# First token group of a four-layer graph network: one uninterrupted run of norm steps, row-sum products behind the first mix, 16 more unread products

## The chip, the cores and the metric

The kernel runs on one core of one Trainium2 chip. The metric is device time in microseconds (us), the median of the runs shown. All tensors are float32.

## The reference

There are 128 graphs of 64 nodes with 256 features each, `x[128, 64, 256]`, and one 64 x 64 matrix `adj` for all. Four layers follow each other; each adds a function of `relu(layernorm(x))` to `x`. Cut to what matters here:

```python
# layer 0: two graph convolutions, then LSTMs over windows of 1, 2, 3 and 4 nodes
h = relu(layernorm(x))
h = relu(einsum('ts,bsh->bth', adj, h @ Wg0 + bg0))
h = relu(einsum('ts,bsh->bth', adj, h @ Wg1 + bg1))
for p in 1..4:
    h[:, every p-th node] = lstm_last(Wih[p-1], Whh[p-1], windows of p nodes of h)
x = x + h
# layer 1: graph convolution with 2*adj/lmax(adj) - I, attention over the nodes, MLP
# layer 2: graph attention; layer 3: two projections between U.T and U,
#          U the eigenvectors of the normalised Laplacian of adj
```

The bias of a graph convolution goes through `adj` too: it reaches an output node multiplied with that node's row sum of `adj`. Layers 1 and 3 need the largest eigenvalue and all eigenvectors of 64 x 64 matrices, which the kernel computes itself.

## The kernel before

**Tiles and groups.** The 8192 node rows are 64 token tiles of 128 rows (two graphs) by 256 features. Layer 0 takes them in 8 groups of 8 tiles (`GT = 8`) and stores each result in DRAM (`put`). Layers 1 to 3 take them in 16 groups of 4 tiles (`HT = 4`). The eigenvalue work (`EIG`, on tiles of `arena`) depends on no tokens and is laid between the groups' work.

**What sets the order.** Every operation is first recorded by a planner (class `Plan`): engine, operands, what it depends on, an estimated cost (`cost`), the group it belongs to, and a `lead` that sets its rank. `schedule` then takes operation after operation, the earliest possible first and by rank among those that are ready, and `issue` writes each engine's program in that order. So every instruction of the program carries the line of `issue`, L349, in the profile, and a changed cost or a changed dependency can re-deal the order of all engines. `plan.burst(cost)` records what stands inside it as one operation, whose instructions stay together. `plan.behind = op` makes everything recorded after it depend on `op`. For operations that lock the port which VectorE and GpSimd share, `schedule` keeps a time of its own (`op.port`).

**How it starts.** The first group's two halves (`X0`, 4 tiles each) are fetched by ACT's DMA queue in pieces of one, one, two, two and two tiles. SP's queue brings `adjT2`, `adj2`, the weights `Wg`, biases and the LSTM's weights `Wih` and `Whh`. TensorE starts with products of a tile of ones with itself, whose results nothing reads: 6 into the bank `warm`, then 8 into the two `seed` banks. In the profile they are `bank<-ones` and `seed<-ones`.

**Row sums.** `rscol` is the row sum of `adj2`, by VectorE. Two products with `adjT2` (`bank<-adjT,ones` and `bank<-adjT,rscol`) put two rows of sums into the bank `rs`; VectorE copies them to `rsrow` and makes `C0T` (two instructions) and `B1T` (four) from them. `C0T` is first needed when a tile pair's second mix is written out, `B1T` after the product with `Wg[1]`.

**Layer 0's front.** The first group goes through in four pairs of tiles (`nl = 2`), the others in fours. For a pair: `ln_stats` (VectorE's `bn_stats` and `bn_aggr`, then four GpSimd instructions that make scale and shift in `stat`), Relu by ACT into `mids`, a mix (16 products of 64 x 64 blocks with `adjTb`, 32 records in the profile), two copies by ACT, four products with `Wg[0]`, a maximum with `nB0` by VectorE (`y`), a second mix, and four additions of `C0T` by VectorE into `big`. Then, for the whole group, eight products with `Wg[1]` (`bank<-big,Wg`, 512 columns), four maxima by VectorE and four additions of `B1T` by GpSimd; the LSTM steps (`bank<-big,Wih`) read their result. In the same time GpSimd makes sums of weight blocks (`sums`), 24 of them, for products that need seven block products in place of eight.

The four GpSimd instructions of `ln_stats` are recorded one by one:

```python
G.tensor_scalar(rs[:, 0, :], mv[:, :, 1], 1e-5, None, op0=ALU.add)
G.tensor_tensor(rs[:, 0, :], rs[:, 0, :], mhalf[:, :n], op=ALU.pow)
G.tensor_tensor(rs[:, 1, :], mv[:, :, 0], rs[:, 0, :], op=ALU.mult)
G.tensor_scalar(rs[:, 1, :], rs[:, 1, :], -1.0, None, op0=ALU.mult)
```

Of the kernel before, what the change touches and what calls it, by code (L numbers as in the profile page):

```python
# [1 line left out]

# [6 lines left out]
ALU = mybir.AluOpType  # L9
# [3 lines left out]
N = 64  # L13
# [55 lines left out]
class Plan:  # L69
# [110 lines left out]
    @staticmethod  # L180
    def cost(op, aps):

        def free(ap):
            n = 1
            for _, c in ap.ap[1:]:
                n *= c
            return n
        n = max(free(a) for a in aps)
        if op.name == "dma_start" and op.eng != "SP":
            return 0.6, 4.0  # L190
        if op.eng == "PE":
            n = free(aps[0])
            if op.name == "transpose":
                c = 0.11
            elif aps[0].ap[0][1] <= 64 and aps[1].ap[0][1] <= 64:
                c = 0.08
            else:
                c = 0.001672 * n + 0.006 if n >= 128 else 0.2
            return c, c + 0.22
        if op.eng == "V":  # L200
            if op.name == "bn_stats":
                c = 0.33
            elif op.name == "bn_aggr":
                c = 0.09
            elif op.name in ("tensor_copy", "tensor_scalar") and all(str(a.space) == "SB" for a in aps):
                c = 0.075 + 0.0006 * n + 0.05 * (len(aps) - 2)
            elif op.name == "reciprocal":
                c = 0.075 + 0.0065 * n
            elif op.name == "tensor_reduce" and aps[1].ap[-1][0] != 1:
                c = 0.075 + 0.0022 * n  # L210
            else:
                c = 0.075 + 0.00105 * n
            if "accum_out" in op.kw:
                c += 0.075
            return c, c + 0.12
        if op.eng == "ACT":
            c = 0.07 + 0.00082 * n + 0.1 * max(0, len(aps) - 2)
            if op.kw.get("func", op.args[2] if len(op.args) > 2 else None) is AF.Exp:
                c += 0.12
            return c, c + 0.15  # L220
        if op.eng == "G":
            c = 0.44 + 0.14 * n if op.kw.get("op") is ALU.pow else 0.12 + 0.00218 * n if n > 64 else 0.2
            return c, c + 0.05
        c = max(0.6, free(aps[0]) * aps[0].ap[0][1] * 4e-6 / 0.39)
        return c, c + 2.2
# [6 lines left out]
    def schedule(self):  # L232
# [20 lines left out]
        while len(order) < len(self.ops):  # L253
# [34 lines left out]
            ready[e].remove(op)  # L288
            tb = self.table(op)
            cost, lat = op.cost, op.lat  # L290
            if tb and tb != table:
                table, cost, lat = tb, cost + 1.29, lat + 1.29
# [603 lines left out]
P = 128  # L896
# [6 lines left out]
SETUP, WEIGHTS, ATTN, REST, EIG = -1, NG, NG + 1, NG + 2, 1000  # L903
# [109 lines left out]
def gnn_kernel(ctx: ExitStack, tc: tile.TileContext, a, out):  # L1013
# [4 lines left out]
    def C(shape, name):  # L1018
        return pool.tile(list(shape), F32, name=name)
# [45 lines left out]
    plan = Plan(tc, {"PE": nc.tensor, "V": nc.vector, "ACT": nc.scalar, "G": nc.gpsimd, "SP": nc.sync}, pools, late, reserve, window, EIG, REST + NT // HT - 6, slack)  # L1065
    PE, V, ACT, G, SP = (plan.proxy(e) for e in ("PE", "V", "ACT", "G", "SP"))

    def bank(name):
        return plan.value("bank")

    def load(t, src):
        SP.dma_start(t, src)
        return t
# [20 lines left out]
    adjT2 = C([P, N], "adjT2")  # L1094
# [9 lines left out]
    bgc = [load(C([P, 2], f"bgc{i}"), a[f"bg{i}"].rearrange("o (c p) -> p (o c)", p=P)) for i in range(2)]  # L1104
# [17 lines left out]
    ones = C([P, P], "ones")  # L1122
    V.memset(ones, 1.0)

    warm = bank("warm")
    for i in range(6):
        PE.matmul(warm[:, :P], ones, ones, start=True, stop=True)
    for i in range(2):
        seed = plan.value("seed")
        for j in range(4):  # L1130
            PE.matmul(seed[:, j * P:(j + 1) * P], ones, ones, start=j == 0, stop=True, skip_group_check=True)
    mhalf = C([P, HT], "mhalf")
    V.memset(mhalf, -0.5)

# [8 lines left out]

    rscol = C([P, 1], "rscol")
    V.reduce_sum(rscol, adj2, axis=AX.X)
    pb = bank("rs")
    PE.matmul(pb[:, :N], ones[:N], adjT2[:N], start=True, stop=True)
    PE.matmul(pb[:, N:2 * N], rscol[:N].to_broadcast([N, P]), adjT2[:N], start=True, stop=True)
    rsrow = C([P, 2, 2, N], "rsrow")
    V.tensor_copy(rsrow, pb[:, :2 * N].rearrange("p (r n) -> p r n", r=2).unsqueeze(2).to_broadcast([P, 2, 2, N]))  # L1150


    V.tensor_scalar(nB0, nB0, rscol, -1.0, op0=ALU.mult, op1=ALU.mult)
    C0T = C([P, 2, P], "C0T")
    B1T = C([P, 2, 2, P], "B1T")
    row = lambda r: rsrow[:, r].rearrange("p r n -> p (r n)")
    for c in range(2):
        V.tensor_scalar(C0T[:, c], row(1), bgc[0][:, c:c + 1], None, op0=ALU.mult)
        for t in range(2):
            V.tensor_scalar(B1T[:, t, c, :], row(0), bgc[1][:, c:c + 1], 1.0 if t else -1.0, op0=ALU.mult, op1=ALU.mult)  # L1160
    G.tensor_tensor(bl, bl, bh, op=ALU.add)


# [95 lines left out]
    def mix(src, m, nt, nc=2):  # L1259

        ps = [bank("mix") for i in range(2)]
        with plan.burst():
            for c in range(nc):
                for t in range(nt):
                    for i, r in ((0, 0), (0, 1), (1, 0), (1, 1)):
                        PE.matmul(ps[i][half(r), bat(c * nt + t)], src(t, c)[half(i), half(r)], m(t)[half(i), half(i)], start=True, stop=True)
        return [p[:, :nc * nt * N].rearrange("p (c t n) -> p c t n", c=nc, t=nt) for p in ps]
# [9 lines left out]
    def mid():  # L1279
        return plan.value("mid")  # L1280
# [8 lines left out]
    def ln_stats(src, n=HT):  # L1289

        s = plan.value("stat")
        st = s[:, :6 * n].rearrange("p (t k) -> p t k", k=6)
        mv = s[:, 6 * n:8 * n].rearrange("p (t k) -> p t k", k=2)
        rs = s[:, 8 * n:10 * n].rearrange("p (k t) -> p k t", k=2)
        for t in range(n):
            V.bn_stats(st[:, t, :], src[:, t, :])
            V.bn_aggr(mv[:, t, :], st[:, t, :])
        G.tensor_scalar(rs[:, 0, :], mv[:, :, 1], 1e-5, None, op0=ALU.add)
        G.tensor_tensor(rs[:, 0, :], rs[:, 0, :], mhalf[:, :n], op=ALU.pow)
        G.tensor_tensor(rs[:, 1, :], mv[:, :, 0], rs[:, 0, :], op=ALU.mult)  # L1300
        G.tensor_scalar(rs[:, 1, :], rs[:, 1, :], -1.0, None, op0=ALU.mult)
        return lambda t: rs[:, 0, t:t + 1], lambda t: rs[:, 1, t:t + 1]


# [106 lines left out]
    def layer0(fetched):  # L1411
# [5 lines left out]
        for t0 in range(0, GT, nl):  # L1417
            sc, bi = norms[t0 // nl]
            two = lambda t: t.rearrange("p (t f) -> p t f", t=2)
            h, ah, y = ([], [], [])  # L1420
            for j in range(0, nl, 2):
                h.append(two(mid()))
                for t in (j, j + 1):
                    ACT.activation(h[-1][:, t - j, :], x[(t0 + t) // HT][:, (t0 + t) % HT, :], AF.Relu, scale=sc(t), bias=bi(t))
            ps = mix(lambda t, c: h[t // 2][:, t % 2, tok(c)], lambda t: adjTb, nl)
            for j in range(0, nl, 2):
                ah.append(mid().rearrange("p (c t) -> p c t", c=2))
                for i in range(2):
                    ACT.copy(ah[-1].rearrange("p c (t b n) -> p c t b n", t=2, b=2)[:, :, :, i, :], ps[i][:, :, j:j + 2, :])
            for j in range(0, nl, 2):  # L1430
                yp = bank("y")
                for t in range(2):
                    for c in range(2):
                        PE.matmul(yp[:, t * D:(t + 1) * D], ah[j // 2][:, c, tok(t)], Wg[0][:, c, :], start=c == 0, stop=c == 1)
                y.append(two(mid()))
                V.tensor_tensor(y[-1], two(yp), vec(nB0, 2), op=ALU.max)
            ps = mix(lambda t, c: y[t // 2][:, t % 2, tok(c)], lambda t: adjTb, nl)
            part = ayT[t0 // HT][:, :, t0 % HT * P:(t0 % HT + nl) * P].rearrange("p c (t b n) -> p c t b n", t=nl, b=2)
            for i in range(2):
                for c in range(2):  # L1440
                    V.tensor_tensor(part[:, c, :, i, :], ps[i][:, c], vec(C0T[:, c, half(i)], nl), op=ALU.add)

        hT = [plan.value("big")[:, :P * GT] for m in range(2)]
        for hf in range(2):
            ts = slice(hf * GT // 2, (hf + 1) * GT // 2)
            for m in range(2):
# [3 lines left out]
                dst = hT[m].rearrange("p (n t) -> p n t", t=GT)[:, :, ts]  # L1450
                b1 = [B1T[:, i, m, :].unsqueeze(2).to_broadcast([P, P, GT // 2]) for i in range(2)]
                V.tensor_tensor(dst, ps.rearrange("p (t n) -> p n t", n=P), b1[0], op=ALU.max)
# [368 lines left out]
```

## Time and profile before

| | |
|---|---|
| median of 3 runs | 2100.99 us (2100.03 to 2101.82) |
| profiled execution | 2099.95 us, span 2098.2 us |
| instructions in the trace | 48166 |
| PE / PEld busy | 2065.2 us (98%) / 1678.8 us (80%) |
| DVE busy | 1767.8 us (84%) |
| ACT busy | 1097.0 us (52%) |
| POOL busy | 777.8 us (37%) |
| mean DMA rate | 28 GB/s |

PE is TensorE, PEld its weight loads, DVE is VectorE, ACT is ScalarE, POOL is GpSimd and SP is SyncE. The span runs from the first to the last instruction; 1.75 us of the execution lie outside it. A row of the timeline has the start in us, the busy time in us, engine, line, operation, what is written and read, shapes, and the number of instructions; in brackets stands how long the engine had been idle before it and what ended that. Buffer numbers are left out of the names, so `bank` is any of the PSUM banks. A matmul of float32 leaves two records. A busy time includes the way through the array, so that the distance between two starts tells more of the rate than a record's length does.

### The profile page before, as it was taken

Reading aid. Unit: us, or ns where it says so; the run is one execution under the profiler, and the core shown is the slowest. Engines: PE = TensorE matmul, PEld = TensorE weight load, DVE = VectorE, ACT = ScalarE, POOL = GpSimd, SP = SyncE. Lnnn points to the kernel's source line nnn. Section 1 sums busy time; section 2 is a strip of 40 time slices with the busy share of each in tenths; the row PEclk is TensorE's granted clock in tenths of the full one; section 3 lists DMA queues with packets and bytes.
Section 4 is the critical chain, followed back from the end, with each engine's and each line's share of the span. In section 5 each row is a group of like instructions: output and inputs, shape, how many; then the busy total and the mean of one; then the engine's idle time right before and its main releaser. Section 6 shows DMA issues by size and latency. Waiting matters only on the chain.

```text
span 2098.2 us, 48166 instructions
## 1 busy us (share of the span) xinstructions
PE 2065.2 (98%) x17928; PEld 1678.8 (80%) x17928; DVE 1767.8 (84%) x6691; ACT 1097.0 (52%) x2465; POOL 777.8 (37%) x1162
## 2 busy tenths in 40 slices
PE   8999999999999999999999999999999999999998
PEld 6689689689779778878878789987887788788776
DVE  7799899899999999999988954877878878885787
ACT  3344544544443453444444435575667666664674
POOL 7422221221211122022010123677557576854354
PEclk9999999999999999999999999999999999999999
DMA  6000100100100100000000211200100100000001
GB/s 231 1 3 3 63 2 2 62 2 2 61 1 1 61 2 1 21 26 2 30 12 1 98 44 33 82 2 1 42 22 1 35 29 22 12 12 11 2 1 62
DMA packets 44875, 57.84 MB, mean 28 GB/s; under 512 B 8928, under 2 KB 38496, under 8 KB 44640
## 3 DMA queue, kind: packets, MB, share of 16 engines
q1 hardware_dynamic: 43536, 53.71, 8.0%
q8 instruction: 141, 2.31, 0.5%
q10 hardware_dynamic: 1104, 1.05, 0.2%
q14 instruction: 94, 0.77, 0.1%
HBM read 37.53 MB, written 16.78 MB: 26 GB/s over the span
## 4 chain that ended last, share of the span: by engine, by line
PE 87%; DVE 10%; issue 1%; ACT 1%; POOL 0%; DMA 0%; DVEq 0%; ACTq 0%
PE bank L349 70%; PE seed L349 17%; DVE big L349 3%; DVE arena L349 3%; DVE stat L349 2%; DVE mids L349 1%; ACT mids L349 1%; DVE sums L349 1%; DMA big<-in_x_dram 0%; DVE seed L349 0%; POOL stat L349 0%; DVE Whh L349 0%; ACT big L349 0%; DVE bank L349 0%; DMA adjT<-in_adjT_dram 0%
## 5 line engine op out<-in xcount | busy, mean ns | idle before, releaser
L349 PE MATMUL bank<-big,Wih 128*128 128x512 f32 (+4 forms) x1800 | 552.1, 425 | 1.1 <-DVE big L349 0.7
L349 PEld LDWEIGHTS bank<-big,Wih 128*128 128x128 f32 x1800 | 315.4, 190 | 141.6 <-issue 95.9
L349 PE MATMUL bank<-big,sums 128*128 128x128 f32 (+3 forms) x1936 | 361.5, 301 | 5.8 <-DVE big L349 2.5
L349 ACT ACTIVATE mids<-bank,bl 128x512 f32<-128x512 f32 (+2 forms) x432 | 246.8, 576 | 206.3 <-PE bank L349 191.9
L349 PE MATMUL bank<-big,Whh 128*128 128x128 f32 (+3 forms) x1304 | 322.5, 333 | 1.4 <-ACT big L349 1.4
L349 PEld LDWEIGHTS bank<-big,sums 128*128 128x128 f32 (+1 forms) x1936 | 286.5, 188 | 40.8 <-issue 17.7
L349 DVE TENSOR_TENSOR arena<-arena 64x42 f32<-64x42 f32 (+6 forms) x1358 | 275.0, 230 | 18.6 <-POOL arena L349 0.3
L349 PEld LDWEIGHTS bank<-big,Whh 128*128 128x128 f32 x1304 | 215.3, 191 | 22.6 <-issue 10.7
L349 ACT ACTIVATE mids<-seed,bl 128x256 f32<-128x256 f32 (+2 forms) x192 | 102.1, 532 | 225.4 <-PE seed L349 223.2
L349 DVE TENSOR_TENSOR big<-mids 128x512 f32<-128x512 f32 (+2 forms) x256 | 154.7, 613 | 27.3 <-ACT mids L349 24.9
L349 POOL TENSOR_SCALAR stat<-stat 128x4 f32<-128x4 f32 (+1 forms) x236 | 70.7, 300 | 260.7 <-DVE stat L349 247.9
L349 PE MATMUL seed<-big,sums 128*128 128x128 f32 (+3 forms) x800 | 141.0, 299 | 0.0
L349 DVE SCALAR_TENSOR_TENSOR arena<-arena 64x1 f32<-64x1 f32 (+16 forms) x565 | 128.7, 251 | 10.6 <-ACT arena L349 3.5
L349 POOL TENSOR_TENSOR big<-big,B1T 128x512 f32<-128x512 f32 x32 | 37.8, 1186 | 255.1 <-DVE big L349 233.8
L349 ACT COPY seed<-bank 128x128 f32<-128x128 f32 (+2 forms) x192 | 53.8, 280 | 145.7 <-PE bank L349 143.8
L349 ACT ACTIVATE mids<-big 128x256 f32<-128x256 f32 (+2 forms) x176 | 89.4, 510 | 74.2 <-DVE big L349 71.5
L349 POOL TENSOR_TENSOR stat<-stat,mhalf 128x4 f32<-128x4 f32 (+1 forms) x118 | 126.2, 1069 | 5.2
L349 ACT COPY mids<-bank 128x256 f32<-128x256 f32 (+3 forms) x320 | 107.6, 357 | 38.7 <-PE bank L349 36.8
L349 POOL MEMSET arena<- 64x2 f32 (+5 forms) x72 | 7.8, 113 | 306.2 <-DVE arena L349 301.7
L349 PEld LDWEIGHTS seed<-big,sums 128*128 128x128 f32 (+1 forms) x800 | 115.8, 189 | 3.5 <-issue 0.3
L349 DVE TENSOR_SCALAR arena<-arena 64x1 f32<-64x1 f32 (+8 forms) x506 | 102.3, 211 | 6.8 <-POOL arena L349 0.3
L349 PE MATMUL seed<-big,Whh 128*128 128x128 f32 (+3 forms) x424 | 103.6, 326 | 0.3 <-DVE big L349 0.3
(507 smaller groups left out, 4615.9 us busy)
## 6 DMA issues: line engine op xcount, KB each, us to landing
big<-in_x_dram SPq DMA_DIRECT2D x29, 512.0 KB, 5.2
put<-big SPq DMA_DIRECT2D x15, 512.0 KB, 3.0
big<-put SPq DMA_DIRECT2D x9, 512.0 KB, 6.4
out_dram<-big SPq DMA_DIRECT2D x18, 256.0 KB, 2.3
Wih<-in_WihT_dram SPq DMA_DIRECT2D x3, 1024.0 KB, 12.0
Whh<-in_WhhT_dram SPq DMA_DIRECT2D x3, 1024.0 KB, 13.6
sums<-put SPq DMA_DIRECT2D x5, 512.0 KB, 4.1
out_dram<-sums SPq DMA_DIRECT2D x10, 256.0 KB, 2.2
```

The source lines that it names most:

```text
L349: getattr(self.engines[op.eng], name)(*map(real, args), **{k: real(a) for k, a in kw.items()})
```

## The change

1. The four GpSimd instructions of `ln_stats` are recorded as one operation in the first group (`plan.burst`, with an estimated cost of 1.04 + 0.14 n us), so that no other GpSimd instruction comes between them.
2. The two row-sum products, the copy to `rsrow` and the six instructions that make `C0T` and `B1T` move into a function `rows()`, which is called once, in the first group, right after the first pair's first mix, and whose operations depend on that mix. The scaling of `nB0` by `rscol` stays where it was.
3. After the 14 unread products 16 more are recorded, into the bank `warm`, with a low rank in group 0.
4. The estimated cost of a DMA that is not issued by SP becomes 0.5 us of issue and a time to landing that grows with its size; before it was 0.6 and 4.0 us for every size.

In the program that the planner makes, the 16 products stand directly behind the 14 and ahead of the first mix.

```diff
--- before.py
+++ after.py
@@ -1,4 +1,4 @@
-from contextlib import ExitStack, contextmanager
+from contextlib import ExitStack, contextmanager, nullcontext
 
 import concourse.bass as bass
 import concourse.tile as tile
@@ -187,7 +187,7 @@
             return n
         n = max(free(a) for a in aps)
         if op.name == "dma_start" and op.eng != "SP":
-            return 0.6, 4.0
+            return 0.5, 1.6 + free(aps[0]) * aps[0].ap[0][1] * 4e-6 / 0.1
         if op.eng == "PE":
             n = free(aps[0])
             if op.name == "transpose":
@@ -1129,6 +1129,10 @@
         seed = plan.value("seed")
         for j in range(4):
             PE.matmul(seed[:, j * P:(j + 1) * P], ones, ones, start=j == 0, stop=True, skip_group_check=True)
+    plan.group, plan.lead = 0, -5
+    for i in range(16):
+        PE.matmul(warm[:, P:2 * P], ones, ones, start=True, stop=True)
+    plan.group, plan.lead = SETUP, 0
     mhalf = C([P, HT], "mhalf")
     V.memset(mhalf, -0.5)
 
@@ -1143,21 +1147,23 @@
 
     rscol = C([P, 1], "rscol")
     V.reduce_sum(rscol, adj2, axis=AX.X)
-    pb = bank("rs")
-    PE.matmul(pb[:, :N], ones[:N], adjT2[:N], start=True, stop=True)
-    PE.matmul(pb[:, N:2 * N], rscol[:N].to_broadcast([N, P]), adjT2[:N], start=True, stop=True)
     rsrow = C([P, 2, 2, N], "rsrow")
-    V.tensor_copy(rsrow, pb[:, :2 * N].rearrange("p (r n) -> p r n", r=2).unsqueeze(2).to_broadcast([P, 2, 2, N]))
-
-
-    V.tensor_scalar(nB0, nB0, rscol, -1.0, op0=ALU.mult, op1=ALU.mult)
     C0T = C([P, 2, P], "C0T")
     B1T = C([P, 2, 2, P], "B1T")
-    row = lambda r: rsrow[:, r].rearrange("p r n -> p (r n)")
-    for c in range(2):
-        V.tensor_scalar(C0T[:, c], row(1), bgc[0][:, c:c + 1], None, op0=ALU.mult)
-        for t in range(2):
-            V.tensor_scalar(B1T[:, t, c, :], row(0), bgc[1][:, c:c + 1], 1.0 if t else -1.0, op0=ALU.mult, op1=ALU.mult)
+
+    def rows():
+
+        pb = bank("rs")
+        PE.matmul(pb[:, :N], ones[:N], adjT2[:N], start=True, stop=True)
+        PE.matmul(pb[:, N:2 * N], rscol[:N].to_broadcast([N, P]), adjT2[:N], start=True, stop=True)
+        V.tensor_copy(rsrow, pb[:, :2 * N].rearrange("p (r n) -> p r n", r=2).unsqueeze(2).to_broadcast([P, 2, 2, N]))
+        row = lambda r: rsrow[:, r].rearrange("p r n -> p (r n)")
+        for c in range(2):
+            V.tensor_scalar(C0T[:, c], row(1), bgc[0][:, c:c + 1], None, op0=ALU.mult)
+            for t in range(2):
+                V.tensor_scalar(B1T[:, t, c, :], row(0), bgc[1][:, c:c + 1], 1.0 if t else -1.0, op0=ALU.mult, op1=ALU.mult)
+
+    V.tensor_scalar(nB0, nB0, rscol, -1.0, op0=ALU.mult, op1=ALU.mult)
     G.tensor_tensor(bl, bl, bh, op=ALU.add)
 
 
@@ -1295,10 +1301,11 @@
         for t in range(n):
             V.bn_stats(st[:, t, :], src[:, t, :])
             V.bn_aggr(mv[:, t, :], st[:, t, :])
-        G.tensor_scalar(rs[:, 0, :], mv[:, :, 1], 1e-5, None, op0=ALU.add)
-        G.tensor_tensor(rs[:, 0, :], rs[:, 0, :], mhalf[:, :n], op=ALU.pow)
-        G.tensor_tensor(rs[:, 1, :], mv[:, :, 0], rs[:, 0, :], op=ALU.mult)
-        G.tensor_scalar(rs[:, 1, :], rs[:, 1, :], -1.0, None, op0=ALU.mult)
+        with plan.burst(1.04 + 0.14 * n) if plan.group == 0 else nullcontext():
+            G.tensor_scalar(rs[:, 0, :], mv[:, :, 1], 1e-5, None, op0=ALU.add)
+            G.tensor_tensor(rs[:, 0, :], rs[:, 0, :], mhalf[:, :n], op=ALU.pow)
+            G.tensor_tensor(rs[:, 1, :], mv[:, :, 0], rs[:, 0, :], op=ALU.mult)
+            G.tensor_scalar(rs[:, 1, :], rs[:, 1, :], -1.0, None, op0=ALU.mult)
         return lambda t: rs[:, 0, t:t + 1], lambda t: rs[:, 1, t:t + 1]
 
 
@@ -1423,6 +1430,10 @@
                 for t in (j, j + 1):
                     ACT.activation(h[-1][:, t - j, :], x[(t0 + t) // HT][:, (t0 + t) % HT, :], AF.Relu, scale=sc(t), bias=bi(t))
             ps = mix(lambda t, c: h[t // 2][:, t % 2, tok(c)], lambda t: adjTb, nl)
+            if plan.group == 0 and t0 == 0:
+                plan.behind = plan.ops[-1]
+                rows()
+                plan.behind = None
             for j in range(0, nl, 2):
                 ah.append(mid().rearrange("p (c t) -> p c t", c=2))
                 for i in range(2):
```

## The prediction

> **What bounds the kernel now.** I read the page from the top: the engines' busy shares, then the 40 slices.
>
> ```profile
> PE 2065.2 (98%) x17928; PEld 1678.8 (80%) x17928; DVE 1767.8 (84%) x6691; ACT 1097.0 (52%) x2465; POOL 777.8 (37%) x1162
> ...
> PE   8999999999999999999999999999999999999998
> ...
> POOL 7422221221211122022010123677557576854354
> ```
>
> TensorE is busy 98% of the span in nearly every slice, so what shortens or empties its queue ahead of the end shortens the run, and any product added to it costs its own time unless it fills a gap. The weak slices are the first and the last. The change stands in the first, so I read the timeline of PE there.
>
> ```profile
> 1.04 2.93 PE L349 MATMUL bank<-ones 128*128 128x128 f32 x12 [1.04 <-DVE ones L349]
> 3.76 3.46 PE L349 MATMUL seed<-ones 128*128 128x128 f32 x16
> 7.15 0.43 PE L349 MATMUL bank<-adjT,ones 64*128 64x64 f32 x2
> 9.12 0.43 PE L349 MATMUL bank<-adjT,rscol 64*128 64x64 f32 x2 [1.54 <-DVE rscol L349]
> 9.48 0.97 PE L349 MATMUL bank<-adjTb,mids 64*64 64x64 f32 x40
> 11.13 0.92 PE L349 MATMUL bank<-adjTb,mids 64*64 64x64 f32 x24 [0.69 <-ACT mids L349]
> ...
> 26.03 0.70 PE L349 MATMUL bank<-Wg,mids 128*128 128x256 f32 x2
> 28.57 0.38 PE L349 MATMUL bank<-arena,ones 128*128 128x1 f32 x2 [1.84 <-DVE arena L349]
> ...
> 37.58 5.42 PE L349 MATMUL bank<-big,Wih 128*128 128x512 f32 x12 [0.39 <-POOL big L349]
> ```
>
> A matmul leaves two records. The 14 unread products (`ones`) end near 7.2 us. Then PE waits 1.54 us for the row sums `rscol`, and the first mix stands behind that wait. PE idles 1.84 us more behind an eigenvalue product, and the LSTM begins at 37.58. From there to 98 us PE is busy 60.14 of 60.42 us: a shift at 37.58 is carried on. The sums by stage add the clock:
>
> ```profile
> 6.92:10.34 3.42, 1.88 (x47) 1.46 (x45) 2.42 (x15) 1.82 (x4) 2.49 (x8) 1.00 0.96 218
> 10.34:17.16 6.82, 6.13 (x45) 5.01 (x38) 4.12 (x26) 3.82 (x9) 4.44 (x11) 0.50 0.96 345
> 17.16:26.70 9.54, 9.54 (x192) 7.45 (x191) 6.17 (x19) 1.59 (x7) 8.49 (x8) 1.00 1.03 412
> ```
>
> After the stage, columns are length, busy time of PE, PEld, DVE, ACT and POOL, then clock. In the stage holding the wait PE is busy 1.88 of 3.42 us, and for the next 6.82 us it runs at half clock: its 128x256 records start 427 ns apart there, 216 ns after 17.16.
>
> **What the Trainium skill says.** "TensorE: Matmul & The Clock Gate", Part 1, "What's actually happening": the array runs at 1.2 GHz until about one window of 3.4 us was busy, at 2.4 GHz then, and falls back after an idle window; windows run freely, whatever the kernel does. The trace agrees in kind: records of `ones` start 213 ns apart up to 6.9 us, and 110 ns apart is the usual value later; the half-clock stage is two windows of 3.41 us. It differs in one point: the window ahead of the fall was not idle, only 55% busy. "SBUF — State Buffer", "two separate sides": VectorE and GpSimd lock one port pair for whole instructions, and a VectorE operation with two SBUF inputs is blocked by a GpSimd one that reads SBUF. The trace agrees: an operation that takes 0.27 us elsewhere takes 3.68 us beside three GpSimd sums without a gap, and the 1.84 us wait of PE above is for it.
>
> ```profile
> 24.72 1.27 POOL L349 TENSOR_TENSOR sums<-sums,Whh 128x512 f32<-128x512 f32 x1
> 24.83 3.68 DVE L349 SCALAR_TENSOR_TENSOR arena<-arena 64x64 f32<-64x64 f32 x1
> ...
> 25.95 1.26 POOL L349 TENSOR_TENSOR Whh<-Whh 128x512 f32<-128x512 f32 x1
> ...
> 27.18 1.26 POOL L349 TENSOR_TENSOR sums<-Whh,sums 128x512 f32<-128x512 f32 x1
> ```
>
> **The change part by part**, with the order of the changed program's instructions laid beside this trace.
>
> *Norm steps in one run.* Today `stat` of the first token pair takes three steps (4.66 to 5.97), and its last one stands behind the first step of the second pair, which waits for tokens until 6.76; so ACT's first Relu starts at 7.33. In one run the four steps need about 0.25 + 0.80 + 0.20 + 0.25 = 1.5 us. VectorE also has the first pair's statistics ahead of the copies into `adjTb` now, some 0.5 us earlier. First Relu about 5.65, first mix's input about 6.75 instead of 8.42. No work is added. The gain is hidden in full, since PE is then still in the unread products.
>
> *16 more unread products.* They stand directly behind the 14. The clock rises at 6.92 in this trace, so they start near 7.0 and take 16 x 2 x 0.110 = 3.5 us: the first mix starts at 10.5, 1.0 us later than today's 9.48. If a window ends at another moment, the end lies between 9.3 and 10.9. Against this the clock should hold: the half-clock stage has 6.13 us of PE work, which takes 3.1 us at full clock.
>
> *Row sums behind the first mix.* Two products (0.36 us of queue), one copy 0.41, two C0T 0.47 and four B1T 0.86 on VectorE; no DMA among them. The wait of 1.54 us goes; what is late next is the unread products. VectorE's copy now waits for the first mix until about 11.7, with eigenvalue steps and the first `y` queued behind it; they would end at 15.3, ahead of PE's need.
>
> *ACT's order.* The copy of the mix's first bank now stands ahead of the second pair's Relus (today one Relu had run before). It waits for the mix until 11.2; then copy 0.37, Relu 0.60, copy 0.36: PE waits from 11.5 to about 12.2 for its first `Wg` product, 0.7 us that today's order did not have. Later ACT runs ahead again.
>
> *The new price of ACT's DMAs* costs nothing itself; it only re-deals the planner's order, on all engines until far into the run.
>
> *Sum.* Following PE's new order from 10.5 with the measured costs (a mix 0.49 us of records plus 0.34 for going in and out; `Wg` 0.43; `Wg` on 512 columns 0.86; eigenvalue products 0.15 to 0.27; waits 0.7 + 0.15 + 0.15) the last product ahead of the LSTM ends at 33.0, today at 37.2: 4.2 us less. GpSimd is the second bound: its weight sums now wait for two eigenvalue steps, to about 16.9 instead of 15.74. Eight sums of 1.25, 1.1 of eigenvalue steps, then three B1T additions of 1.11 with two sums between: 16.9 + 10.0 + 1.1 + 3.3 + 2.5 = 33.8, which frees the LSTM's first product. 37.58 - 33.8 = 3.8, and I take this. Going between 64-row and 128-row products costs 0.17 us each; the new order has 173 such changes against 177, at most one of them counted above: 0.5 less. Both together 4.3; I round to 4.0, as one short wait for the port is likely. The profiled execution took 2099.95 (span 2098.2, 1.75 outside it) and would take 2096; the median of the three runs stands 1.0 higher, at 2100.99: **2097.0**. Unknown costs: the eigenvalue waits in the new order, 0 to 3.7 us; the clock, 0 to 1.7 (one more half-clock window); the re-dealt rest, where PE has waits of 0.5 to 2.2 us at some 25 places, -3 to +3.
>
> **The rivals.**
> 1. *Clock falls anyway* (0.10). The window from 10.3 to 13.75 then holds 64-row products, the 0.7 us wait and 1.5 us of `Wg`; today's 55% was too little. Then 1.7 us are lost, and a port stall near today's 1.84 takes most of the rest: 2100. For it: the same kind of gap as today; against: today's gap lay in a window with 0.3 us of full products.
> 2. *More is gained* (0.16). No port stall in the first group, and the re-dealt order meets fewer waits later (for VectorE 2.2 at 261 us, 1.5 at 783, 1.6 at 1230): 4.3 + 3.5, 2093.
> 3. *Slower* (0.22). The unread products fill no gap, since the mix's input is there at 6.75, so they are 3.5 us of pure queue; and in the new order eigenvalue products stand in PE's queue ahead of group work while their VectorE steps wait at the locked port. Today one such wait cost 1.84. It decides from two full stalls of 3.7 on: 3.6 us eat the gain, and 5 more from further waits until 100 us (PE's stalls there are 7 us per 50 already) make 2106. For it: GpSimd's six sums without a gap; against: the planner sets port use apart.
> 4. *Nothing is moved* can be excluded for the start: the order shows it. That the gain is given back at the end is unlikely: the tail's order is the same.
>
> **How the numbers follow.** Main case 0.52, own range 2094.5 to 2100; 0.2% is 4.2 us, about what a measurement of this kernel can tell from no change, and cuts the main case near its middle. Faster: 0.26 + 0.16 = 0.42. Same: 0.26 + 0.09 of the first rival = 0.35. Slower: 0.22 + 0.01. The range from 2090.5 to 2106.5 takes in all but the tails of rivals 2 and 3.
>
> **What would show it.** First Relu near 5.7; `ones` until 10.5; clock 1.00 from 6.9 on, with no half-clock stage; first `Wg` near 12.2; 128x256 records 216 ns apart from the start; the LSTM's first product near 34. A half-clock stage after 13 us, or a VectorE step of over 3 us ahead of an eigenvalue product, would make it wrong.

## The result, and the profile after

The changed kernel takes **2091.11 us**, the median of five runs (2090.27 to 2091.66); the kernel before took 2100.99 beside it, the median of five (2098.51 to 2102.20). The ratio is 0.9952, 95% interval 0.9941 to 0.9962, so the change saves 9.9 us. The forecast was 2097.0 with a range of 2090.5 to 2106.5: the measured time lies 5.9 us below the forecast and 0.6 us inside the lower end. The profiled execution took 2091.66 (span 2089.9), 8.3 us less than that of before.

From the page of the changed kernel, the busy shares and the slices of PE:

```profile
PE 2064.4 (99%) x17960; PEld 1682.9 (81%) x17960; DVE 1760.6 (84%) x6691; ACT 1095.7 (52%) x2465; POOL 776.0 (37%) x1162
...
PE   9999999999999999999999999999999999999998
```

PE has 32 records more and as much busy time as before; the first slice is no longer its weak one. The timeline of PE in the changed kernel, as in the prediction (start, busy time, what, and in brackets the idle time ahead and what ended it):

```profile
3.76 3.05 PE L349 MATMUL seed<-ones 128*128 128x128 f32 x16
6.64 3.74 PE L349 MATMUL bank<-ones 128*128 128x128 f32 x32
10.31 0.69 PE L349 MATMUL bank<-adjTb,mids 64*64 64x64 f32 x32
...
11.21 0.39 PE L349 MATMUL bank<-adjT,rscol 64*128 64x64 f32 x2
12.22 2.00 PE L349 MATMUL bank<-Wg,mids 128*128 128x256 f32 x8 [0.63 <-ACT mids L349]
...
34.23 7.13 PE L349 MATMUL bank<-big,Wih 128*128 128x512 f32 x16 [0.21 <-POOL big L349]
```

The 16 unread products (x32) end at 10.3, the row-sum product no longer waits, and the LSTM begins at 34.23 instead of 37.58. In the sums by stage of the changed kernel (length, busy time of PE, PEld, DVE, ACT, POOL, then clock) no stage of the front runs at half clock:

```profile
6.06:10.31 4.25, 4.25 (x39) 4.13 (x37) 2.41 (x14) 0.87 (x2) 2.90 (x9) 1.00 0.75 213
10.31:17.16 6.85, 5.95 (x148) 5.29 (x148) 5.19 (x24) 4.89 (x12) 3.46 (x8) 1.00 1.01 355
17.16:26.70 9.54, 9.10 (x132) 7.33 (x131) 7.47 (x32) 1.00 (x5) 8.90 (x10) 1.00 1.03 411
```

The clock of this execution falls once later, for 3.41 us at 2050.64; in before's profiled execution it holds there.

In the timeline of DVE and POOL of the changed kernel the eigenvalue step that was locked for 3.68 us before is back, at 23.48:

```profile
15.82 1.74 DVE L349 TENSOR_TENSOR arena<-arena 64x1 f32<-64x1 f32 x1 [0.20 <-POOL arena L349]
16.28 1.26 POOL L349 TENSOR_TENSOR sums<-Wih 128x512 f32<-128x512 f32 x1
...
23.48 0.53 DVE L349 SCALAR_TENSOR_TENSOR arena<-arena 64x64 f32<-64x64 f32 x1
...
33.08 1.11 POOL L349 TENSOR_TENSOR big<-big,B1T 128x512 f32<-128x512 f32 x1
```

It takes 0.53. A shorter lock of 1.74 has come at 15.82. The addition of `B1T` at 33.08 is the third, and it releases the LSTM's first product at 34.23.

**Where the time went**, by the start of the same products in both profiled executions: at the LSTM's first product the changed kernel is 3.35 us ahead; at layer 1's first product (`lapb`; 1283.67 before, 1276.78 after) 6.89; at the last product 8.29. So the front gave 3.35, the long stretch from the LSTM to layer 1 gave 3.54, and layers 1 to 3 gave 1.40. PE's waits from 34 to 1290 us, first of before and then of the changed kernel (us in total, times, the longest; the three largest groups of each):

```profile
PE bank L349 <- DVE big L349: 3.2, 6, 1.2
PE bank L349 <- DVE arena L349: 3.0, 5, 1.6
PE bank L349 <- DVE seed L349: 2.5, 4, 1.2
...
```

```profile
PE bank L349 <- DVE seed L349: 3.8, 6, 1.2
PE bank L349 <- DVE arena L349: 2.5, 7, 0.5
PE bank L349 <- DVE big L349: 1.5, 4, 0.6
...
```

With the smaller groups they sum to 10.5 and 8.3 us: some 2.2 of the 3.54 us are these waits. About 1.0 us more is PE's busy time in the stretch (1235.1 us before, 1234.1 in the changed kernel), and the rest lies in shorter gaps. No single wait carries it. The 1.40 us of the end are not counted as the change's: the order of PE there is the same in both programs, and in two executions of one order (the changed kernel, and below the one without its unread products) this stretch takes 808.8 and 812.7 us, with single PE stalls of 0.9 to 1.7 us that no recorded event ends.

### The profile page after: what moved, and what is told of

Read it like the earlier page. It is cut to its first block, busy times and chain, and to the rows that moved or that the text cites. A ratio compares the mean times of both kernels' runs of the same rounds, so it can differ in the third digit from the quotient of the medians.

```text
span 2089.9 us, 48219 instructions
## 1 busy us (share of the span) xinstructions
PE 2064.4 (99%) x17960; PEld 1682.9 (81%) x17960; DVE 1760.6 (84%) x6691; ACT 1095.7 (52%) x2465; POOL 776.0 (37%) x1162
## 3 DMA queue, kind: packets, MB, share of 16 engines
q10 hardware_dynamic: 1104, 1.05, 0.2%
## 4 chain that ended last, share of the span: by engine, by line
PE 90%; DVE 8%; ACT 1%; issue 1%; POOL 0%; DVEq 0%; ACTq 0%
PE bank L349 73%; PE seed L349 17%; DVE arena L349 3%; DVE big L349 2%; DVE stat L349 1%; DVE mids L349 1%; DVE sums L349 1%; ACT mids L349 0%; POOL stat L349 0%; DVE seed L349 0%; DVE Whh L349 0%; ACT big L349 0%; ACT arena L349 0%; ACT sums L349 0%; POOL big L349 0%
## 5 line engine op out<-in xcount | busy, mean ns | idle before, releaser
L349 DVE TENSOR_TENSOR big<-mids 128x512 f32<-128x512 f32 (+2 forms) x256 | 149.2, 590 | 26.2 <-ACT mids L349 23.1
L349 DVE SCALAR_TENSOR_TENSOR arena<-arena 64x1 f32<-64x1 f32 (+16 forms) x565 | 130.4, 253 | 10.3 <-ACT arena L349 4.1
L349 POOL TENSOR_TENSOR big<-big 128x128 f32<-128x128 f32 (+2 forms) x48 | 30.5, 634 | 198.0 <-DVE big L349 120.0
```

The source lines that it names most:

```text
L349: getattr(self.engines[op.eng], name)(*map(real, args), **{k: real(a) for k, a in kw.items()})
```

## The experiments

Each ratio is to the kernel before on the same chip (its medians there: 2102.25, 2101.90 and 2101.45 us for the three sets of four). It is taken over all executions, so that it can differ from the ratio of the medians. "LSTM" is the start of its first product in the profiled execution, 37.58 before and 34.23 after.

A trace shows one execution, and executions of one program differ in how long TensorE ran at half clock. The mean granted clock is on record for each; 0.001 less of it is about 4.2 us at half clock (an estimate: twice 0.001 of 2100 us). The time goes with it (mean us of the executions at each mean clock, and how many; 0.996 and 0.997 are left out):

| kernel | 0.999 | 0.998 | 0.995 |
|---|---|---|---|
| before, 107 executions in the three sets | none | 2100.7 (39) | 2103.0 (20) |
| `b_front`, 13 | 2097.7 (2) | 2099.5 (5) | 2105.5 (1) |
| `b_unread`, 13 | 2096.4 (2) | 2098.8 (5) | 2103.5 (2) |
| `b_sum`, 16 | 2096.8 (5) | 2101.7 (9) | none |
| `a_drop`, 5 | 2091.5 (2) | 2094.7 (3) | none |
| the changed kernel, 5 | 2091.0 (4) | 2091.1 (1) | none |

So a ratio near 1 can be a mean over executions that gained and others that did not. And at one and the same mean clock of 0.998 the changed kernel's single execution is 9.6 us below the mean of before's: its gain is not only the clock.

### First set: which part of the change is it

**b_front: the three named edits in the old order.** Before's planned order; the 16 products behind the 14, each norm step directly behind the one before it, the row-sum products with `C0T` and `B1T` behind the first mix:

```diff
+        for a, b in self.pairs:
+            order.remove(a)
+            order.insert(order.index(b) + 1, a)
...
+        at = order.index(self.first_mix) + 1
+        return order[:at] + rows + order[at:]
...
+                if op is self.last_seed:
+                    for i in range(16):
+                        self.engines["PE"].matmul(real(self.warm[:, P:2 * P]), real(self.ones), real(self.ones), start=True, stop=True)
```

> The order of the kernel before on every engine, with the three edits of the front put into it by hand and nothing else moved: 16 unread products behind the 14, the first group's norm steps in one run, the row sums with C0T and B1T behind the first mix. Theory A (the front gives 3 to 4 us, the rest of the gain comes from the re-dealt order after it): first LSTM product near 34.5, time about 2097.5. Theory B (the whole gain follows from the earlier start, and the order does nothing): first LSTM product near 34.2 and time 2091 to 2093. If ACT's order matters (here one Relu of the second pair stands ahead of the copy, as before), the first Wg product comes near 11.6 instead of 12.2.

Measured: 2100.16 us, ratio 0.9996 (0.9988 to 1.0004): no change on the average. LSTM at 38.56, later than before. From the timeline of b_front, DVE and then PE:

```profile
23.25 4.60 DVE L360 SCALAR_TENSOR_TENSOR arena<-arena 64x64 f32<-64x64 f32 x1
```

```profile
27.92 0.38 PE L360 MATMUL bank<-arena,ones 128*128 128x1 f32 x2 [2.76 <-DVE arena L360]
```

GpSimd's sums stand back to back from 20.40 to 27.77, the eigenvalue step is locked for 4.60 us, PE waits 2.76, and the clock falls for 3.41 us at 28.50. The row-sum wait was removed, the first `Wg` product came at 11.78, and in this execution all of it was lost behind the locked step. In the two executions at 0.999 it was not: they took 2097.6 and 2097.8 us, as theory A had it, 3 us less than before's at 0.998. No trace of them was kept.

**b_unread: only the 16 products in the old order.** The last three lines of the diff above.

> The order of the kernel before with only the 16 unread products put in behind the 14. They end near 10.3, then come the row sums and the first mix at 10.9 instead of 9.5. If the products are worth what the clock says: no half-clock stage, 3.1 us won against 1.4 lost, LSTM near 35.9, time 2099.3. If they are only added queue: time 2102 or more. If the clock falls all the same: 2104.

Measured: 2099.87 us (2094.79 to 2103.63), ratio 0.9993 (0.9984 to 1.0001). From the timeline of DVE, POOL and PE in b_unread:

```profile
15.88 2.49 POOL L349 TENSOR_TENSOR sums<-Wih 128x512 f32<-128x512 f32 x2
16.45 3.22 DVE L349 SCALAR_TENSOR_TENSOR arena<-arena,ident 64x64 f32<-64x64 f32 x1
18.34 1.25 POOL L349 TENSOR_TENSOR sums<-sums,Wih 128x512 f32<-128x512 f32 x1
...
19.73 0.43 PE L349 MATMUL bank<-arena 128*128 128x64 f32 x2 [2.40 <-DVE arena L349]
```

The products end at 10.85, the DVE step is locked for 3.22 us, PE waits 2.40, and the clock stays at half for 10.24 us from 20.83: in this execution they don't keep it up. It is one of the longer ones (2103.13), with LSTM at 41.92. The two at a mean clock of 0.999 took 2094.79 and 2098.05; none of the 107 executions of before is below 2098.18. So the products can be worth some us, and in this order they are not so on the average.

**a_drop: the changed kernel's order without the 16 products.**

```diff
+                if op in self.unread:
+                    continue
```

> The order of the changed kernel on every engine, with the 16 unread products left out. If they do nothing but hold the clock: the first mix starts near 7.0 instead of 10.3, the clock falls to half near 10 for two windows, 3.1 to 3.4 us are lost there, and the time stays within 1 us of the changed kernel, 2091. If the clock holds without them, PE reaches the LSTM up to 3 us earlier but GpSimd's sums bound it: 2089 to 2090. If more waits come with the fall: 2093 to 2094.

Measured: 2093.78 us, ratio 0.9958 (0.9945 to 0.9970), which overlaps the changed kernel's interval. The timeline of PE in a_drop:

```profile
6.67 0.84 PE L351 MATMUL bank<-adjTb,mids 64*64 64x64 f32 x32
...
9.33 0.68 PE L351 MATMUL bank<-adjT,rscol 64*128 64x64 f32 x2 [1.45 <-DVE rscol L351]
...
34.16 6.28 PE L351 MATMUL bank<-big,Wih 128*128 128x512 f32 x14 [0.18 <-POOL big L351]
```

The first mix starts 3.6 us earlier than in the changed kernel. PE then waits 1.45 for the row sums, and it runs at half clock from 9.34 to 12.75. The LSTM starts at 34.16, and the addition of `B1T` that releases it at 33.00 (33.08 in the changed kernel). GpSimd's queue sets the end of the front with and without the unread products. Up to layer 1 (1276.49, in the changed kernel 1276.78) they cost nothing and bring nothing; the 3.6 us by which this profiled execution (2095.25) is longer are stalls of PE in layers 1 to 3 that no event ends.

**b_cost: only the new price for DMAs that SP does not issue.**

```diff
-            return 0.6, 4.0
+            return 0.5, 1.6 + free(aps[0]) * aps[0].ap[0][1] * 4e-6 / 0.1
```

> The kernel before with only the new price of ACT's DMAs, which re-deals the planner's order and changes no work. Theory A: the time moves by up to 4 us either way, by waits of PE after 38 us. Theory B: it stays within 1 us of 2101.

Measured: 2094.69 us, ratio 0.9962 (0.9950 to 0.9975). By the ratio that is 8.0 us of the 9.9, from an estimate that executes nothing. The timeline of PE in b_cost:

```profile
6.47 1.07 PE L349 MATMUL bank<-adjTb,mids 64*64 64x64 f32 x32
8.94 0.43 PE L349 MATMUL bank<-adjT,rscol 64*128 64x64 f32 x2 [1.40 <-DVE rscol L349]
...
31.61 1.98 PE L349 MATMUL bank<-big,Wih 128*128 128x512 f32 x4 [0.45 <-POOL big L349]
```

Its first mix stands ahead of the row-sum wait, its longest DVE step in the front takes 1.02 us, and its clock does not fall in the front: LSTM at 31.61, 2.6 us earlier than in the changed kernel.

### Second set: is it the price, and is it the lock

**a_oldcost: all three edits planned with the old price.** The line above put back in the changed kernel.

> The changed kernel with all three named edits, but planned with the old estimate of 0.6 and 4.0 us for DMAs that SP does not issue. The planner deals a third order. Theory A (the new price's order makes the gain): most of the gain goes, 2097 to 2102. Theory B (the three named edits make it): 2089 to 2093. Theory C (any re-dealing moves the time by several us, whatever the price): anything, and then the front shows where: the longest VectorE step beside GpSimd sums and PE's waits ahead of the LSTM say whether it was the port again.

Measured: 2091.69 us, ratio 0.9960 (0.9947 to 0.9974), LSTM at 33.61: the same gain. So the price isn't needed either, once the planner is free to deal the edits a new order. Counted back from layer 1's first product, TensorE's records name the same tiles in the same order as in the changed kernel over 8302 of the 8480 records that lie between it and the LSTM's first; in b_cost over 7840; in the kernel before over 284. Three different causes led to nearly one later order.

**b_price5: the price wrong the other way.** Before with `return 0.6, 5.0`.

> The kernel before with only the estimate of non-SP DMAs changed, from 4.0 us to landing to 5.0, further from the trace's own landing times than before. Theory A (a price nearer to the real landing gives a better order, a worse one a worse order): 2101 to 2106. Theory B (a changed price only re-deals, better or worse by luck, and the old order was an unlucky one): 2092 to 2099, with VectorE's longest step in the front near 1 us. Theory C (the orders are the same but for a few instructions): 2100 to 2102.

Measured: 2105.01 us, ratio 1.0015 (1.0009 to 1.0022), LSTM at 38.85. It has a later order of its own (284 records as in the changed kernel), 1.8 us longer from LSTM to layer 1 than before. By the ratios a DMA price can take 8.0 us or add 3.2. The right-price theory agrees with this run, but a_oldcost, with the wrong price and the full gain, doesn't need it.

**b_later and a_later: GpSimd's sums out of the front.** The weight sums ahead of the first group's last `B1T` addition are moved behind it, in before's order and in the changed kernel's:

```diff
+        at = max(order.index(op) for op in self.b1t)
+        sums = [op for op in order[:at] if op in self.sums]
+        order = [op for op in order if op not in sums]
+        at = max(order.index(op) for op in self.b1t) + 1
+        return order[:at] + sums + order[at:]
```

> The kernel before, its order written out as planned, except that GpSimd's weight sums that stood ahead of the first group's last B1T addition are moved behind it in the issue order. Theory A (the front's lost time is VectorE's eigenvalue steps locked out beside back-to-back GpSimd sums): the VectorE step of 3.68 us at 24.83 takes 1.0 or less, PE's wait of 1.84 us behind it and the 0.39 us wait for B1T go, the half-clock stage stays where it is; LSTM's first product near 35 instead of 37.58, and the time 2098.5 to 2099.5. Theory B (what the front gains is taken back by later waits for the sums, or the order elsewhere decides): LSTM near 35 but 2101 to 2103. Theory C (GpSimd has no room for the sums later): a product with seven blocks waits for its sums, over 2103.

> The changed kernel with the same move of the weight sums behind the first group's last B1T addition. Theory A: GpSimd stops being the second bound of the front; the 1.74 us VectorE step at 15.82 takes 0.5, the LSTM's first product comes near 33.2 instead of 34.23, set by PE's own queue, and the time is 1 us below the changed kernel's: ratio to before near 0.9948. Theory B: no difference from the changed kernel (0.9952), since the later waits take it back. Theory C: sums come late, 1 to 3 us more than the changed kernel.

Measured: b_later 2116.78 us, ratio 1.0069 (1.0057 to 1.0082); a_later 2105.11, ratio 1.0016 (1.0009 to 1.0023): by the ratios 14.5 and 3.4 us over before. The front does what theory A says: no DVE step over 0.69 us in its first 40 us, LSTM at 35.25 (though this execution waited 2.56 for `rscol`, 1.0 more than before) and 33.50. Then, from the timeline of PE in b_later:

```profile
56.53 0.48 PE L357 MATMUL bank<-adjTb,mids 64*64 64x64 f32 x4 [10.33 <-ACT mids L357]
```

The second group's norm steps stood behind the moved sums on GpSimd (37.18 to 57.19), so ACT's Relu and PE's mix came 10 us late, and the clock was at half for 17.07 us from 46.88 on (in a_later 13.65 us from 47.75). It was theory C with another victim than I had named: not the products that use the sums, but the next group's tokens. For a_later the size was missed too: theory C had 1 to 3 us over the changed kernel, and it took about 14 us more.

### Third set: can the gain be put together by hand

**b_gap: only the three sums that lock the step give way.** GpSimd's power step, which waits for that step, goes ahead of them, and all later sums stand three places down; the second group's norm steps keep their places:

```diff
+        for op in order[order.index(out[0]):]:
+            if op in out:
+                continue
+            new.append(next(line) if op in self.sums else op)
+            if op is last:
+                new += [next(line) for _ in out]
```

> The kernel before in its own order, except that three of GpSimd's weight sums (those at 24.72, 25.95 and 27.18 us) give their places up: the power step that waits for VectorE's eigenvalue step moves ahead of them, each later sum stands three places down, and the second group's norm steps keep their places ahead of the last three. Theory A (lock-out behind gapless sums): VectorE's 3.68 us step takes 0.6 or less, PE's wait of 1.84 us goes, LSTM's first product at 35.4 to 36.4 instead of 37.58 with the half-clock stage still there, second group without the 10 us wait of the coarser move; 2099 to 2100. Theory B (the step was late for another reason): the step moves or stays long, LSTM at 37.0 or later, 2101 to 2103.

Measured: 2103.16 us, ratio 1.0009 (1.0001 to 1.0017). From the timeline of DVE and PE in b_gap:

```profile
25.41 0.21 DVE L369 SCALAR_TENSOR_TENSOR arena<-arena 64x64 f32<-64x64 f32 x1
...
52.13 1.25 DVE L369 TENSOR_SCALAR arena<-arena 64x64 f32<-64x64 f32 x1 [4.05 <-POOL arena L369]
...
53.52 0.41 PE L369 MATMUL bank<-arena 128*128 128x64 f32 x2 [3.29 <-DVE arena L369]
```

The step that took 3.68 us takes 0.21, PE's wait behind it is gone, and the LSTM starts at 36.06, 1.5 earlier. That is the lock, shown by taking it away. Then the next power step of the eigenvalue work (51.52) finds the deferred sums ahead of it, VectorE waits 4.05 and PE 3.29: 17 us later more is given back than was won.

**b_front_gap: the three edits in the old order, with the same step-down.** Both edits above.

> The three named edits spliced into the order of before (as in the first of these runs), plus the same step-down of three weight sums. Theory A: the edits' gain in the front was eaten by a 4.60 us locked step, PE's 2.76 us wait and the fall of the clock behind it; without the lock the LSTM starts at 33.8 to 34.8 instead of 38.56 with no half-clock stage ahead of it, the rest stays as before, and the time is 2096 to 2098, ratio near 0.9975. Theory B (the edits bring nothing even so): LSTM at 36 or later, 2099 to 2101.

Measured: 2105.61 us (2099.43 to 2109.97), ratio 1.0017 (1.0008 to 1.0026), LSTM at 39.20. From the timeline of DVE, POOL and PE in b_front_gap:

```profile
15.36 4.03 DVE L380 TENSOR_SCALAR arena<-ident,arena 64x64 f32<-64x64 f32 x1
15.64 2.48 POOL L380 TENSOR_TENSOR sums<-Wih 128x512 f32<-128x512 f32 x2
18.09 1.26 POOL L380 TENSOR_TENSOR sums<-sums,Wih 128x512 f32<-128x512 f32 x1
...
19.54 0.66 PE L380 MATMUL bank<-arena,ones 128*128 128x64 f32 x2 [2.92 <-DVE arena L380]
```

This lock isn't the one that was removed. The same step took 0.25 us in b_front, at 14.77, with the sums starting at 16.17; here it came 0.6 us later and the sums 0.5 us earlier, with the same order of instructions up to there. So in this order the moment at which steps and sums meet differs between executions, and the 13 runs lie 10.5 us apart; the five of the changed kernel lie 1.4 apart, the five of a_oldcost, with nearly the same order, 5.7.

**b_rest: before's front, and the later order that the new price makes.** Both orders are planned; the first is kept up to the LSTM's first product:

```diff
+        front, rest = (old, new) if self.front_old else (new, old)
+        at = next(i for i, op in enumerate(front) if op is self.lstm)
+        front = front[:at]
+        kept = set(front)
+        order = self.schedule(front + [op for op in rest if op not in kept])
```

(`front_old` is true here.)

> The kernel before with its own order up to the LSTM's first product, and from there the order that the planner makes with the new price for non-SP DMAs (nearly the changed kernel's from 100 us on). Theory A (the later order is worth something by itself): LSTM at 37.6 as before, from there to layer 1 2.0 to 3.5 us less, 2097.5 to 2099.5. Theory B (it pays only behind the front that it was dealt for): the same or longer from LSTM to layer 1, 2101 to 2104.

Measured: 2102.53 us, ratio 1.0005 (0.9996 to 1.0013). From the LSTM's first product to layer 1 it takes 3.8 us less than before. But the LSTM starts at 42.21, 4.6 us late. The new order has two more eigenvalue products ahead of it; behind the old front the step for them comes late, and PE waits 2.61 at 41.74. The clock also fell a second time in this front, for 3.41 us at 29.92. Counted from the front's last `Wg` product (36.61 before, 38.54 here), 1.1 us are left. The later order pays only in small part behind a front that it was not dealt for.

**b_sum: all pieces by hand.** The edits of b_front_gap and b_rest together.

> All pieces put together by hand: the three named edits in the order of before, the step-down of three weight sums, and from the LSTM's first product the order that the new price makes. Theory A (the pieces add): LSTM at 33.8 to 34.8 as in the run without the later order, LSTM to layer 1 2 to 3.5 us less, 2092 to 2095, near the changed kernel's 2091. Theory B (they do not add; the planner's orders hang together): waits behind the join, 2096 to 2100.

Measured: 2101.20 us (2096.46 to 2103.98), ratio 0.9995 (0.9988 to 1.0002). In its profiled execution, a short one, no lock of 4 us fell in the front and the clock held, yet LSTM is at 36.64 behind a 2.88 us wait for the same two eigenvalue products, and layer 1 begins 2.5 us ahead of before. On the average the pieces don't add. But the 16 executions fall into two lots: six took 2096.5 to 2098.4 us, less than any of the 44 of before beside them (2098.57 or more), and ten took 2101.0 to 2104.0. In the short lot about half of the gain is there.

## Why the prediction was right, and where it was not

**The front: right in its places.** First Relu 5.65 forecast, 5.83 measured; unread products until 10.5, measured 10.3; first `Wg` product 12.2, measured 12.22; sums from 16.9, measured 16.28; LSTM 33.8, measured 34.23. The last is partly luck: GpSimd's chain began 0.6 us earlier than forecast and took 1.05 us longer (17.95 us for 16.9). GpSimd was named as the second bound and is the one that ends the front: a_drop shows it, where PE's front is quite different and the LSTM starts 0.07 us away.

**The term that was mis-sized: "the re-dealt rest, -3 to +3", taken at nil.** The prediction said that the new price "costs nothing itself; it only re-deals the planner's order". That is so, but the re-dealing was the larger thing: -3.54 us between LSTM and layer 1 against nothing in the sum, just outside the bound. By the median the gain was 9.9 where the main case said 4.0. The second rival had the size (2093), and its reasons in kind: no step locked over 1.74 us in the first group, and PE's waits of 1.58 and 1.17 us at 263 and 785 us gone, though one of 1.19 came at 308. It lies 1.9 us over the measured 2091.1, less than the last stretch varies between executions. Two readings behind the rivals were off. PE's waits in before are 1.58, 1.17 and 1.23 us where the second rival has 2.2, 1.5 and 1.6. And the third rival's stalls of 7 us per 50 until 100 us are not there: PE is idle 0.97 us between 50 and 100, 5.49 between 0 and 50.

**The cause given for the front: only partly right.** The prediction let the named edits make the front's gain: the row-sum wait of 1.54 gone, the clock held by the unread products (3.1 us). b_front has those edits and on the average no gain (3 us in the two executions at 0.999); a_drop lacks the unread products, loses the clock for 3.41 us, and has the gain. What ends the front is GpSimd's chain of sums, eigenvalue steps and `B1T` additions, and how VectorE's steps fall between the sums. The 3.1 us were hidden behind that chain in the changed kernel's order. The 3.8 us of the forecast came near the measured 3.35 because they were taken from GpSimd's chain and not from PE's; the 0.5 us added to them, for fewer changes between 64-row and 128-row products, can't be told apart in the traces.

**The third rival (slower) had a mechanism that exists.** Eigenvalue products in PE's queue behind a locked VectorE step cost 2.40 us in b_unread, 2.76 in b_front and 2.92 in b_front_gap, as it said. The changed kernel escaped it, with a longest lock of 1.74 us. Of six orders around the old front (b_front, b_unread, b_gap, b_front_gap, b_rest, b_sum) none is faster than before on the average beyond its interval.

**What stays open.** Three plans (edits and price, price alone, edits alone) reach nearly one later order and about the same time; no single instruction or wait was found whose move gives the 9.9 us. Locks in the front explain 1.5 us in b_gap; the later order gave 1.1 to 3.8 of the stretch behind the front in b_rest; the hand-made sum of both gave, on the average, nothing that can be told from no change. The executions of b_front, b_unread and b_sum in which the clock held took 2096.4 to 2097.7 us in the mean, 3 to 4 us less than before and 5 to 7 more than the changed kernel: the named edits may be worth that much where no lock and no half-clock step follow. This was read off the spread of executions and not tested by an edit. Why the planner falls into this order from three sides, and not from the price of 5.0, was not tested. Nor were the first and the second edit tried singly under the planner.

## What to carry to other kernels

Where a planner deals the order, an edit is two changes: what it does, and what order it brings. Splice the edit into the old order, and re-deal the order without it, before you believe that the edit was the cause. Forecast the re-dealing as a term of its own, as wide as other re-dealt orders of the kernel lie apart (here -10 to +3 us), and look at the engine that ends the stage: a wait removed from another engine's queue is hidden there. Where executions differ in their clock, one trace is one draw: read the spread of the times beside it.

## What the runs showed of the hardware

- **A lock can last over several instructions, and need not.** A VectorE step of 0.21 to 0.27 us took 3.22, 3.68, 4.03 and 4.60 us beside GpSimd sums of 1.25 us without a gap between them, and ended when that run of sums did. The Trainium skill, "SBUF — State Buffer", "Who interferes with whom", has the pair held for one whole instruction by whoever issues first. The runs agree on the blocking, but in these four cases the wait was the length of three to four sums. (In b_front_gap VectorE's record began 0.28 us ahead of the first sum's, while a GpSimd power step was under way.) Other steps were let in after one sum, though the next followed without a gap. The step of 3.22 us in b_unread took 0.27 in the kernel before (16.83), beside the same sums, and 1.23 in b_gap:

```profile
15.93 2.50 POOL L369 TENSOR_TENSOR sums<-Wih 128x512 f32<-128x512 f32 x2 [0.76 <-DMA Wih<-in_WihT_dram]
17.28 1.23 DVE L369 SCALAR_TENSOR_TENSOR arena<-arena,ident 64x64 f32<-64x64 f32 x1
...
18.37 1.29 POOL L369 TENSOR_TENSOR sums<-sums,Wih 128x512 f32<-128x512 f32 x1
```

  What decides between one sum and several is open.
- **The clock changes in steps of 3.41 us, and it falls after a step in which PE was little busy.** In all 14 traces every change lies a whole number of 3.413 us behind the first clock record, and the stretches at half clock are 3.41, 6.83, 10.24, 13.65 and 17.07 us long. There are 24 falls ahead of the last product. In the step just before them PE was busy 0 to 58%; each step at full clock with 46% or less was followed by a fall, none with more than 58% was, and between these both occur. So a gap counts by how it lies in the steps. Around gaps of 1.45 us (a_drop) and 1.40 us (b_cost), first of a_drop and then of b_cost (length, busy time of PE, PEld, DVE, ACT, POOL, then clock):

```profile
5.93:9.34 3.41, 1.96 (x42) 1.58 (x41) 2.12 (x13) 2.35 (x6) 1.76 (x6) 1.00 0.80 235
9.34:12.75 3.41, 3.41 (x9) 2.75 (x10) 3.14 (x21) 1.62 (x4) 2.91 (x8) 0.50 0.86 234
```

```profile
4.39:7.80 3.41, 2.91 (x49) 2.37 (x47) 2.08 (x10) 1.68 (x4) 2.11 (x5) 1.00 0.94 298
7.80:11.22 3.42, 2.28 (x10) 1.73 (x10) 3.30 (x19) 1.61 (x5) 2.49 (x8) 1.00 0.88 177
```

  In a_drop the gap lies in one step, 57% busy, and the clock falls. In b_cost a border between steps divides it, the two are 85% and 67% busy, and the clock holds. The first clock record lies anywhere from 3.93 to 7.18 us in the 14 executions, so the same gap can cost the clock in one execution and not in the next.
- **PE stalls with no releaser.** In layers 1 to 3 PE has one to four stalls in each profiled execution that no event in the records ends, 0.9 us in all in the changed kernel and 4.5 in a_drop with the same order. They were not expected, and their cause is open.
